# Cross-attention over sixteen batches: the attention product of eleven batches in seven block products, with its sums on GpSimd, and the softmax maximum as bias of the exponential

## The chip, the core and the metric

The kernel runs on one core of a Trainium2 chip. The engines are named as in the profile: PE (TensorE, matmuls), PEld (its weight loads), DVE (VectorE), ACT (ScalarE), POOL (GpSimd) and SP (SyncE, which only issues transfers here). PE writes its results to PSUM, which has eight banks; POOL does not touch PSUM. The metric is device time in microseconds (us), the median of several runs.

## The reference

Everything is in 32-bit floating point. There are 16 batches, 256 queries of 256 features, 77 keys of 192 features, 8 heads of width 256.

```python
Q = (img_embed @ Wq).reshape(B, -1, H, D).transpose(0, 2, 1, 3)
K = (sent_embed @ Wk).reshape(B, -1, H, D).transpose(0, 2, 1, 3)
V = (sent_embed @ Wv).reshape(B, -1, H, D).transpose(0, 2, 1, 3)
score = jnp.einsum('bhqd,bhkd->bhqk', Q, K) / math.sqrt(D)
score = jnp.where(mask, score, -jnp.inf)
attn = jax.nn.softmax(score, axis=-1)
ctx = jnp.einsum('bhqk,bhkd->bqhd', attn, V).reshape(B, -1, H * D)
out = ctx @ Wo + img_embed
mu = jnp.mean(out, axis=-1, keepdims=True)
var = jnp.var(out, axis=-1, keepdims=True)
return (out - mu) * jax.lax.rsqrt(var + EPS) * gamma + beta
```

## The kernel before

**What is multiplied.** The weights are folded once: Wq and Wk of each head into gA and gB (the 192 context features are split into 128 and 64, hence A and B), Wv and Wo into uA and uB. Per group of four batches, g is applied to the context (tiles `pa` in PSUM, copied to `a`), and the scores of a batch are x times a (`ps`). Per batch, u is applied to the context (`pv`, copied to `vw`), and the output is the attention weights times vw (`po`), added to x. Of the 77 keys of a head, 64 go through vw; the last 13 of all heads are packed into one more block, `vr`.

**How it is tiled.** A batch has two tiles of 128 queries; a tile is numbered t, a batch b. Nearly all matmuls in the loop use 32 output columns of the array, so that four of them, one for each quarter of the output's partitions, run together; each is executed in two passes, and the profile counts passes. `attend` (L357) makes `po` of a tile from five terms, four blocks of 128 weights (`pT`, turned by DVE's transpose in `turn`) against 256 columns of vw and one against vr.

**The softmax of a tile.** `shift` (L306): two DVE additions of the mask bias to `ps` give s, a DVE maximum gives top, and POOL subtracts top from s. `exponential` (L324): one ACT exponential of 128x616. `weigh` (L329): a DVE sum and reciprocal, then two POOL multiplications into p (128x512 and 128x104). `turn` (L347): a DVE transpose into pT.

**The layer norm of a tile.** `finish` (L371): DVE adds po to x in place and takes the statistics. `spread` (L383): ACT's square root, which needs another function table than the exponential. `invert` (L390): DVE's reciprocal. `normalise` (L403): two DVE instructions (L416 with gamma, L419 with beta), or, put aside, one on ACT and two on POOL; after the second tile of a batch SP issues the transfer of the output.

**The order.** It is written out by hand: each engine executes its instructions in program order, with semaphores between engines. The loop is software-pipelined over b from -1. An iteration computes the scores of batch b+1 (`new`), prepares vw of b+1 and, up to b = 10, a quarter of the a of the next group, attends for batch b (`now`) and finishes and normalises batch b-1 (`old`). On PE the order is scores, part A of the preparations, part B, attend. On DVE it is finish of old, shift of new, (a transpose of vr), reciprocal, then per tile the sum and the normalisation of an old one, transposes of x in half of the iterations, and turn. On ACT it is the square root, then exponential and copies alternately, then the rest of the copies. All PSUM tiles come from one ring of eight banks (`ps_mm`), taken in program order; an iteration with a takes 4 + 2 + 4 + 2 of them, and a bank is taken again when its reader has let go.

**Set-up.** Before the loop, u is folded from Wv and Wo (`pu`, `pw`), POOL copies four pieces of uB to the other half of the partitions, and after them makes the mask bias ready, for which all shifts wait.

Of the kernel before, what the change touches and what calls it, by code (L numbers as in the profile page):

```python
# [8 lines left out]
F32 = mybir.dt.float32  # L9
I32 = mybir.dt.int32  # L10
AF = mybir.ActivationFunctionType
ALU = mybir.AluOpType
AX = mybir.AxisListType
PSUM = bass.MemoryType.PSUM

P = 128
H = 8
D = 256
EPS = 1e-05
GB = 4  # L20
KM = 64
MASKED = 3.0e38

# [19 lines left out]
def kernel(  # L45
# [13 lines left out]
    nc = tc.nc  # L59
    B, S, DI = x.shape  # L60
    S2, DL = c.shape[1], c.shape[2]
# [3 lines left out]
    NG = B // GB  # L65
# [31 lines left out]

    gB = const.tile([P, NF, DI], F32, tag="gB", name="gB")

    uA = const.tile([P, 2, DI // BK, NF, BK], F32, tag="uA", name="uA")  # L100
    uB = const.tile([P, 2, DI // BK, NF, BK], F32, tag="uB", name="uB")

    cA = const.tile([P, B, S2], F32, tag="cA", name="cA")
    cB = const.tile([P, B, S2], F32, tag="cB", name="cB")
# [16 lines left out]
    def flat(ap):  # L121
        return ap.rearrange("p a b -> p (a b)")

    def half(i):
        return slice(i * LB, (i + 1) * LB)
# [31 lines left out]
    def transpose_x(g, j):  # L157

        cols = xT_of[g][:, j * NM : (j + 2) * NM]
        nc.vector.transpose(cols, cols)  # L160
# [54 lines left out]

    def prepare_vw(b):

        vw_of[b] = vwp.tile([P, 2, 2, DI], F32, tag="vw", name=f"vw_{b}", bufs=3)
        pv = []

        def part_A():
            for k in range(2):
                pv.append(ps_mm.tile([P, 2 * DI], F32, tag="mm", name=f"pv_{b}_{k}"))
                for i in range(NM):
                    nc.tensor.matmul(  # L225
                        pv[k][i * BK : (i + 1) * BK],
                        cA[:, b, k * BK : (k + 1) * BK],
                        uA[:, :, :, i],
                        start=True,
                        stop=False,  # L230
                    )

        def part_B():
            for i in range(NM):
                for k in range(2):
                    nc.tensor.matmul(  # L236
                        pv[k][i * BK : (i + 1) * BK],
                        cB[half(k), b, k * BK : (k + 1) * BK],
                        uB[half(k), :, :, i],
                        start=False,  # L240
                        stop=True,
                    )

        def copies():
            return [
                (vw_of[b][:, :, k, :], pv[k].rearrange("p (e d) -> p e d", e=2)) for k in range(2)
            ]

        return part_A, part_B, copies

    def prepare_last():


        pr = [ps_mm.tile([P, 2, B, KR], F32, tag="mm", name=f"pr_{n}") for n in range(DI // BK)]

        def part_A(e):
            for n, o in enumerate(pr):
                nc.tensor.matmul(  # L258
                    o[:, e].rearrange("p b k -> p (b k)"),
                    flat(uA[:, e, n]),  # L260
                    flat(cRA),
                    start=(e == 0),
                    stop=(e == 1),
                )

        def part_B(e):
            for n, o in enumerate(pr):
                nc.tensor.matmul(  # L268
                    o[:, e].rearrange("p b k -> p (b k)"),
                    flat(uB[half(n % 2), e, n]),  # L270
                    flat(cRB[half(n % 2)]),
                    start=(e == 1),
                    stop=(e == 0),
                )

        part_A(0)
        part_B(0)
        part_B(1)
        part_A(1)
        for n, o in enumerate(pr):  # L280
            to = vr[:, :, n * BK : n * BK + 2 * KR]
            evacuate(to.rearrange("p b (e k) -> p e b k", e=2), o)
# [22 lines left out]

    def shift(t):  # L306

        b, ps = t // QT, ps_of.pop(t)
        s = sp.tile([P, H, S2], F32, tag="s", name=f"s_{t}")
        for a in range(2):  # L310
            nc.vector.tensor_tensor(  # L311
                s[:, a * H // 2 : (a + 1) * H // 2],
                ps[a][:, : H // 2 * S2].rearrange("p (h k) -> p h k", k=S2),
                bias[:, b, :].unsqueeze(1).to_broadcast([P, H // 2, S2]),
                ALU.add,
            )
        top = st.tile([P, H], F32, tag="top", name=f"top_{t}")
        nc.vector.tensor_reduce(top, s, AX.X, ALU.max)  # L318
        nc.gpsimd.tensor_tensor(  # L319
            s, s, top.unsqueeze(2).to_broadcast([P, H, S2]), ALU.subtract  # L320
        )
        s_of[t] = s

    def exponential(t):  # L324
        e = sp.tile([P, H, S2], F32, tag="e", name=f"e_{t}")
        nc.scalar.activation(e, s_of.pop(t), AF.Exp)  # L326
        e_of[t] = e

    def weigh(t):  # L329
# [27 lines left out]
    def attend(t):  # L357
        b, pT = t // QT, pT_of.pop(t)
        po = ps_mm.tile([P, DI], F32, tag="mm", name=f"po_{t}")
        for n in range(NF + 1):  # L360
            for i in range(NM):
                nc.tensor.matmul(  # L362
                    po[i * BK : (i + 1) * BK],
                    pT[:, n, i],
                    vw_of[b][:, n // 2, n % 2, :] if n < NF else vr[:, b, :],
                    start=(n == 0),
                    stop=(n == NF),
                )
        po_of[t] = po

    def finish(t):  # L371
        g, j = t // GT, t % GT
        y = xg_of[g][:, j, :]
        nc.vector.tensor_tensor(y, po_of.pop(t), y, ALU.add)
        bn = st.tile([P, 6], F32, tag="bn", name=f"bn_{t}")
        nc.vector.bn_stats(bn, y)
        if j == 0:
            mv_of[g] = st.tile([P, GT, 2], F32, tag="mv", name=f"mv_{g}", bufs=2)
        nc.vector.bn_aggr(mv_of[g][:, j, :], bn)  # L379
# [3 lines left out]
    def spread(first, last):  # L383

        g, lo, hi = first // GT, first % GT, (last - 1) % GT + 1
        std = st.tile([P, GT], F32, tag="std", name=f"std_{first}")
        nc.scalar.activation(std[:, lo:hi], mv_of[g][:, lo:hi, 1], AF.Sqrt, bias=eps)  # L387
        std_of[first, last] = std
# [45 lines left out]
    with tc.tile_pool(name="wonce", bufs=1) as wp:  # L434
# [32 lines left out]
            load_blocks(wq_blk[:, e], wq_blocks[2 * e + 1])  # L467
        load_c(first, NCR)

        warm = wp.tile([P, 1], F32, tag="warm", name="warm")  # L470
        nc.scalar.activation(warm, eps, AF.Exp)

        wvT = wp.tile([P, NF, NL, P], F32, tag="wvT", name="wvT")
# [208 lines left out]
        for j in range(NF // 2):  # L682
            pu = two_banks("pu", j)
            for a in range(2 * j, 2 * j + 2):
                of_pair(pu, a, wv_part, wo_part)
            for e in range(2):
                evacuate(
                    uA[:, e, :, 2 * j : 2 * j + 2].rearrange("p n a c -> p a n c"),
                    pu[e].rearrange("p a (n c) -> p a n c", c=BK),
                )  # L690
        for j in range(NF // 2):
            for e, pw in enumerate(
                rest_of_pairs(j, (2 * j, 2 * j + 1), wv_part, wo_part, "pw")
            ):
                for i, engine in enumerate((nc.scalar.copy, nc.vector.tensor_copy)):
                    a = 2 * j + i
                    here, there = uB[half(i), e, :, a], uB[half(1 - i), e, :, a]
                    engine(here, pw[half(i)].rearrange("p (n c) -> p n c", c=BK))
                    nc.gpsimd.tensor_copy(there, here)
        nan = wp.tile([P, B, 1], F32, tag="nan", name="nan")  # L700
        nc.vector.tensor_reduce(nan[:, :, 0], bias, AX.X, ALU.max)
        nc.gpsimd.tensor_tensor(nan, nan, nan, ALU.mult)
# [16 lines left out]
    for b in range(-1, B):  # L719
# [2 lines left out]
        new = range((b + 1) * QT, min(b + 2, B) * QT)  # L722
        for t in new:
            scores(t)
        if old and new:
            for t in old:
                finish(t)
            spread(old[0], old[-1] + 1)
        for t in new:
            shift(t)  # L730
        for n in range(0, 2) if b < 0 else range(b + 2, min(b + 3, B // 2)):
            turn_last(n)
        if old and new:
            invert(old[0], old[-1] + 1, aside=b >= B - GB - 1)
        g, n = (b + 1) // GB + 1, (b + 1) % GB
        work = []
        if b + 1 < B:
# [8 lines left out]
        for _, part_B, _ in work:  # L746
            part_B()
        copies = [copy for _, _, of_part in work for copy in of_part()]
        for i, t in enumerate(new):
            exponential(t)  # L750
            for dst, src in copies[i : i + 1]:
                nc.scalar.copy(dst, src)  # L752
        for dst, src in copies[len(new) :]:
            nc.scalar.copy(dst, src)  # L754
        for i, t in enumerate(new):
            weigh(t)
            if old and b < B - 2 and (i or b < B - GB - 1):
                normalise(old[i])
        if g < NG and n >= NF - 2:
            for j in range((n - NF + 2) * GT // 2, (n - NF + 3) * GT // 2, 2):  # L760
                transpose_x(g, j)
        for t in now:
            attend(t)
        for t in new:
            turn(t)
        if B - GB - 1 <= b < B - 2:
            normalise(old[0], aside=True)
        if b == B - 2:
            for i in range(QT):
# [46 lines left out]
```

## Time and profile before

| | us |
|---|---|
| median of 3 runs | 288.15 (286.89 to 288.93) |
| the profiled execution | 285.98 |
| its span, first to last instruction | 284.2 |
| set-up on PE, until the first scores | 57.3 |
| an iteration with a (b = 1 to 10) | 14.5 |
| an iteration without a (b from 11) | 11.4 |
| after the last gap-free matmul, to the end | 16 |

In the profile's rows, a line such as L362 is a line of the kernel, `po<-vw,pT` names the tile written and those read, `128*32` is the rows and columns of the array in use, and `x1024` counts instructions (passes on PE). The second number of a row is the busy time of the group, then the mean of one; the number after the next bar is the time that the engine sat idle before it. In the chain of waits each piece is followed back to what released it. In the table of windows each engine has its busy time and its count.

Other rows that matter, by line and form (busy us, mean ns): the POOL subtraction L319, 128x616, 38.9 and 1216; POOL's products for p, L340, 128x512, 35.4 and 1107; the exponential L326, 23.0 and 719; the 128x512 copies to vw, L752, 18.6 and 581; the 128x308 copies to a, L754, 16.6 and 447.

### The profile page before, as it was taken

Reading aid. Unit: us, or ns where it says so; the run is one execution under the profiler, and the core shown is the slowest. Engines: PE = TensorE matmul, PEld = TensorE weight load, DVE = VectorE, ACT = ScalarE, POOL = GpSimd, SP = SyncE. Lnnn points to the kernel's source line nnn. Section 1 sums busy time; section 2 is a strip of 40 time slices with the busy share of each in tenths; the row PEclk is TensorE's granted clock in tenths of the full one; section 3 lists DMA queues with packets and bytes.
Section 4 is the critical chain, followed back from the end, with each engine's and each line's share of the span. In section 5 each row is a group of like instructions: output and inputs, shape, how many; then the busy total and the mean of one; then the engine's idle time right before and its main releaser. Section 6 shows DMA issues by size and latency. Waiting matters only on the chain.

```text
span 284.2 us, 11523 instructions
## 1 busy us (share of the span) xinstructions
PE 274.4 (97%) x5221; PEld 180.2 (63%) x5221; DVE 215.3 (76%) x421; ACT 115.2 (41%) x199; POOL 119.1 (42%) x150
## 2 busy tenths in 40 slices
PE   8999999999999999999999999999999999999990
PEld 7746599976474747575656565666656567476550
DVE  0245953775777989988888888897978898898883
ACT  3303222214362444453535353535353534725541
POOL 1000069524515252525252434352533437748574
PEclk9999999999999999999999999999999999999998
DMA  6997999960000105920101039301010101010112
GB/s 211 229 224 174 325 213 225 155 142 2 2 6 2 40 2 102 189 86 5 39 2 40 2 81 193 105 2 39 3 39 5 40 3 39 2 42 3 39 40 74
DMA packets 35634, 22.51 MB, mean 79 GB/s; under 512 B 17712, under 2 KB 34048, under 8 KB 35584
## 3 DMA queue, kind: packets, MB, share of 16 engines
q1 hardware_dynamic: 35584, 21.77, 34.8%
q8 instruction: 41, 0.67, 1.0%
q14 instruction: 9, 0.07, 0.1%
HBM read 17.57 MB, written 4.19 MB: 77 GB/s over the span
## 4 chain that ended last, share of the span: by engine, by line
PE 93%; DVE 2%; POOL 1%; ACT 1%; issue 1%; POOLq 0%
PE ps L297 24%; PE po L362 22%; PE pa L184 12%; PE pv L225 10%; PE pa L198 6%; PE pv L236 6%; PE pu L568 3%; PE pr L258 2%; PE pg L611 1%; PE idle L493 1%; PE pw L582 1%; PE pgb L568 1%; PE pr L268 1%; PE pc L545 1%; PE phb L582 1%; PE ph L625 1%
## 5 line engine op out<-in xcount | busy, mean ns | idle before, releaser
L319 POOL TENSOR_TENSOR s<-s,top 128x616 f32<-128x616 f32 x32 | 38.9, 1216 | 90.5 <-DVE top L318 86.0
L297 PE MATMUL ps<-a,xT 128*32 128x154 f32 x2048 | 70.0, 294 | 0.0
L297 PEld LDWEIGHTS ps<-a,xT 128*32 128x32 f32 x2048 | 66.4, 110 | 3.5 <-issue 0.7
L340 POOL TENSOR_TENSOR p<-e,rden 128x512 f32<-128x512 f32 x64 | 50.1, 802 | 31.8 <-ACT a L754 27.0
L362 PE MATMUL po<-vw,pT 128*32 128x256 f32 x1024 | 61.5, 380 | 0.0
L362 PEld LDWEIGHTS po<-vw,pT 128*32 128x32 f32 x1024 | 31.8, 110 | 28.2 <-issue 5.5
L332 DVE TENSOR_REDUCE den<-e 128x8 f32<-128x616 f32 x32 | 25.3, 790 | 23.6 <-ACT e L326 23.6
L184 PE MATMUL pa<-cA,gA 128*32 128x308 f32 x512 | 35.8, 423 | 0.4 <-ACT cA L136 0.4
L326 ACT ACTIVATE e<-s 128x616 f32<-128x616 f32 x32 | 23.0, 719 | 28.7 <-POOL s L319 28.7
L752 ACT COPY vw<-pv 128x512 f32<-128x512 f32 x32 | 18.6, 581 | 36.1 <-PE pv L236 36.1
L311 DVE TENSOR_TENSOR s<-ps,bias 128x308 f32<-128x308 f32 x64 | 27.8, 465 | 4.1 <-PE ps L297 4.1
L225 PE MATMUL pv<-uA,cA 128*32 128x512 f32 x256 | 30.4, 592 | 0.0
L184 PEld LDWEIGHTS pa<-cA,gA 128*32 128x32 f32 x512 | 16.4, 110 | 21.1 <-issue 6.1
L419 DVE SCALAR_TENSOR_TENSOR xg<-xg,rstd,bet 128x256 f32<-128x256 f32 x25 | 27.9, 1117 | 0.9
L387 ACT ACTIVATE std<-mv,eps 128x2 f32<-128x2 f32 (+1 forms) x17 | 5.0, 296 | 55.1 <-DVE mv L379 54.3
L350 DVE STREAM_TRANSPOSE pT<-p 128x640 f32<-128x640 f32 x32 | 25.0, 811 | 2.5 <-POOL p L340 2.5
L318 DVE TENSOR_REDUCE top<-s 128x8 f32<-128x616 f32 x32 | 25.5, 796 | 1.1
L362 PE MATMUL po<-vr,pT 128*32 128x256 f32 x256 | 19.7, 379 | 0.0
L198 PE MATMUL pa<-cB,gB 64*32 64x308 f32 x512 | 19.5, 420 | 0.0
L387 ACT ACT_TABLE_LOAD x15 | 19.2, 1283 | 0.3
L326 ACT ACT_TABLE_LOAD x14 | 18.0, 1283 | 0.3
L236 PE MATMUL pv<-uB,cB 64*32 64x512 f32 x256 | 17.4, 601 | 0.0
(86 smaller groups left out, 272.2 us busy)
## 6 DMA issues: line engine op xcount, KB each, us to landing
xT<-in_x_dram SPq DMA_DIRECT2D x16, 256.0 KB, 7.4
xg<-in_x_dram SPq DMA_DIRECT2D x4, 1024.0 KB, 9.0
out_dram<-xg SPq DMA_DIRECT2D x15, 256.0 KB, 2.2
wo<-in_L_xattn_Wo_dram SPq DMA_DIRECT2D x4, 512.0 KB, 5.4
wvT<-in_L_xattn_Wv_dram SPq DMA_DIRECT2D x16, 96.0 KB, 3.9
wq_nat<-in_L_xattn_Wq_dram SPq DMA_DIRECT2D x2, 512.0 KB, 6.1
wq_blk<-in_L_xattn_Wq_dram SPq DMA_DIRECT2D x8, 128.0 KB, 4.4
wk_blk<-in_L_xattn_Wk_dram SPq DMA_DIRECT2D x8, 96.0 KB, 5.8
```

Source lines behind the costliest of these rows:

```text
L184: nc.tensor.matmul(flat(o[i * BK : (i + 1) * BK]), gA[:, h, cols(dc, i)], flat(cA[:, batches, :]), start=not B_first, stop=B_first,)
L198: nc.tensor.matmul(flat(banks[j + k][i * BK : (i + 1) * BK]), gB[half(k), h % NF, cols(dc, i)], flat(cB[half(k), batches, :]), start=B_fir ...
L225: nc.tensor.matmul(pv[k][i * BK : (i + 1) * BK], cA[:, b, k * BK : (k + 1) * BK], uA[:, :, :, i], start=True, stop=False,)
L236: nc.tensor.matmul(pv[k][i * BK : (i + 1) * BK], cB[half(k), b, k * BK : (k + 1) * BK], uB[half(k), :, :, i], start=False, stop=True,)
L297: nc.tensor.matmul(ps[m // 2][i * BK : (i + 1) * BK, m % 2 * 2 * S2 : (m % 2 + 1) * 2 * S2], xT_of[g][:, j * NM + m, dc], flat(a_of[g][:, ...
L311: nc.vector.tensor_tensor(s[:, a * H // 2 : (a + 1) * H // 2], ps[a][:, : H // 2 * S2].rearrange("p (h k) -> p h k", k=S2), bias[:, b, :]. ...
L318: nc.vector.tensor_reduce(top, s, AX.X, ALU.max)
L319: nc.gpsimd.tensor_tensor(s, s, top.unsqueeze(2).to_broadcast([P, H, S2]), ALU.subtract)
L326: nc.scalar.activation(e, s_of.pop(t), AF.Exp)
L340: nc.gpsimd.tensor_tensor(part, e_mh[:, :, :, keys], rden_mh.unsqueeze(3).to_broadcast(list(part.shape)), ALU.mult,)
L362: nc.tensor.matmul(po[i * BK : (i + 1) * BK], pT[:, n, i], vw_of[b][:, n // 2, n % 2, :] if n < NF else vr[:, b, :], start=(n == 0), stop= ...
L419: nc.vector.scalar_tensor_tensor(y, y, rstd, bet, ALU.mult, ALU.add)
```

## The change

For batches 0 to 10 the two tiles of a batch are multiplied together. Attention weights (two tiles by two halves of the heads) and vw (two halves of the heads by two halves of the output features) are both cut into two by two blocks, and the product is taken by Winograd's form of Strassen's scheme: seven block products instead of eight, and sums before and after.

- Set-up: u gets a fifth block, the combination t2 = b22 - b12 + b11, by four POOL additions of 128x512 placed ahead of the bias. `vw` has four blocks of 128 columns: t2, b21, b22, b11 for these batches, and b21, b22, b11, b12 for the others, at the same 512 columns of matmul.
- `differences` (POOL, one instruction of 128x768) makes t4, t1, t3 of a batch from vw. `sums` (POOL, four of 128x256) makes s1 to s4 from the turned weights.
- `seven` replaces `attend`: four products into bank `pm`, three products and the last keys into bank `po`, all with 128 columns; ACT then copies pm to `m`.
- `add_seven`: DVE adds po to x (moved here from `finish`), and POOL adds m into m twice (128x128) and m into x three times (128x256).
- Softmax, batches 0 to 11: the maximum is taken negated, POOL's subtraction is gone, and the exponential is eight instructions of 128x77, one for each head, with the maximum as bias.
- Order in iterations -1 to 10: DVE takes the shift of new first, and the statistics of old between the sums of new; ACT takes both tiles' exponentials, then the square root, then the copies, the copy of pm, and a small exponential that brings the table back; on DVE then follow the reciprocal, the normalisation of the first old tile, turn, the transposes of x, the normalisation of the second old tile and the additions of po; on POOL p, differences, the additions of m, sums.

```diff
+    def differences(b):
+        vw = vw_of[b].rearrange("p q k d -> p q (k d)")
+        ts = vwp.tile([P, 3, 2, P], F32, tag="ts", name=f"ts_{b}", bufs=2)
+        nc.gpsimd.tensor_tensor(
+            ts.rearrange("p q k d -> p q (k d)"),
+            vw[:, 1:4],
+            vw[:, 0:1].to_broadcast([P, 3, 2 * P]),
+            ALU.subtract,
+        )
+    def sums(b):
...
+        nc.gpsimd.tensor_tensor(s1, a2[0], a2[1], ALU.add)
+        nc.gpsimd.tensor_tensor(s3, a2[0], a1[0], ALU.subtract)
+        nc.gpsimd.tensor_tensor(s2, a2[1], s3, ALU.add)
+        nc.gpsimd.tensor_tensor(s4, a1[1], s2, ALU.subtract)
+    def seven(b):
...
+        def contract(out, *terms):
+            for n, (weight, moving) in enumerate(terms):
+                for i in range(NM):
+                    nc.tensor.matmul(
+                        out[i * BK : (i + 1) * BK],
+                        weight[:, i],
+                        moving,
+                        start=(n == 0),
+                        stop=(n == len(terms) - 1),
+                    )
...
+        contract(pm[:, 0], *block(pT[0][:, 0:2], b11))
+        contract(pm[:, 1], *block(s2, t2))
+        contract(pm[:, 2], *block(s3, t3))
+        contract(pm[:, 3], *block(s1, t1))
+        contract(po[:, 0], *block(pT[0][:, 2:4], b21), last[0])
+        contract(po[:, 1], *block(s4, b22), last[1])
+        contract(po[:, 2], *block(pT[1][:, 2:4], t4), last[2])
+        contract(po[:, 3], last[3])
...
+        nc.scalar.copy(m, pm)
+    def add_seven(b):
...
+        for i in range(QT):
+            add_product(QT * b + i)
+        add(m[:, 1], m[:, 0])
+        add(m[:, 2], m[:, 1])
+        add(y[:, 0], m[:, 0:2])
+        add(y[:, :, 1], m[:, 3:4].to_broadcast([P, QT, P]))
+        add(y[:, 1], m[:, 2:3].to_broadcast([P, 2, P]))
...
-        nc.vector.tensor_reduce(top, s, AX.X, ALU.max)
-        nc.gpsimd.tensor_tensor(
-            s, s, top.unsqueeze(2).to_broadcast([P, H, S2]), ALU.subtract
-        )
+        nc.vector.tensor_reduce(top, s, AX.X, ALU.max, negate=t // QT <= NS)
...
-        nc.scalar.activation(e, s_of.pop(t), AF.Exp)
+            for h in range(H):
+                nc.scalar.activation(e[:, h], s[:, h], AF.Exp, bias=top[:, h : h + 1])
...
+        for u in (uA, uB):
+            t2, _, b22, b11, b12 = (u[:, q].rearrange("p n i c -> p (n i c)") for q in range(5))
+            nc.gpsimd.tensor_tensor(t2, b22, b12, ALU.subtract)
+            nc.gpsimd.tensor_tensor(t2, t2, b11, ALU.add)
...
+        if b < NS:
+            for i, t in enumerate(new):
+                exponential(t)
+                if old:
+                    finish(old[i])
+                weigh(t)
+            if old:
+                spread(old[0], old[-1] + 1)
+            for dst, src in copies:
+                nc.scalar.copy(dst, src)
+            if b + 1 < NS:
+                differences(b + 1)
+            if now:
+                seven(b)
+            nc.scalar.activation(warm, eps, AF.Exp)
+            if old:
+                invert(old[0], old[-1] + 1)
+                normalise(old[0])
+            for t in new:
+                turn(t)
+            if n >= NF - 2:
+                for j in range((n - NF + 2) * GT // 2, (n - NF + 3) * GT // 2, 2):
+                    transpose_x(g, j)
+            if old:
+                normalise(old[1])
+            if now:
+                add_seven(b)
+            if b + 1 < NS:
+                sums(b + 1)
+            continue
```

## The prediction

> **What bounds the kernel now.** I read the page's busy table and 40 slices first, then the chain of waits in order of time, then one loop iteration by engine.
>
> ```profile
> PE 274.4 (97%) x5221; PEld 180.2 (63%) x5221; DVE 215.3 (76%) x421; ACT 115.2 (41%) x199; POOL 119.1 (42%) x150
> ...
> PE   8999999999999999999999999999999999999990
> ...
> DVE  0245953775777989988888888897978898898883
> ```
>
> PE is busy 97% of the span; DVE is next and, inside the loop, near full. A busy PE may still be waiting within its rows, so the chain of waits in order of time decides (start, us, what):
>
> ```profile
> 125.56 4.19 PE ps L297 x128
> 129.74 1.72 PE pv L225 x16
> 131.46 2.07 PE pa L184 x32
> 133.53 1.02 PE pv L236 x16
> 134.55 1.04 PE pa L198 x32
> 135.59 4.45 PE po L362 x80
> 140.04 4.19 PE ps L297 x128
> ```
>
> Each piece begins where the one before ended. One iteration is scores 4.19, preparation 5.85, attend 4.45: 14.48 us, and the chain stays on PE from 16.5 to 268 us. So in the loop a microsecond of matmul is a microsecond of time, and other engines cost nothing until PE waits for them. Their room in one such iteration, from the table of windows:
>
> ```profile
> core 0: us, PE busy (x) PEld busy (x) DVE busy (x) ACT busy (x) POOL busy (x), PEclk, DMA share, GB/s
> 130.00:144.48 14.48, 14.48 (x309) 9.01 (x305) 12.11 (x25) 6.53 (x11) 5.67 (x7) 1.00 0.06 20
> ```
>
> The clock is full (1.00). DVE has 2.4 us to spare, ACT 8, POOL 8.8.
>
> **The change part by part.**
>
> *PE, batches 0 to 10 (the forecast's gain).* A product here is two passes over four column tiles that run together; I call one pass of four a round. Old attend: 2 tiles x 5 terms x 2 passes = 20 rounds of 256 columns (the x80 above). New: seven block products of 2 terms, plus four last-key terms, 18 terms x 2 passes = 36 rounds of 128 columns. Columns fall from 20x256 = 5120 to 36x128 = 4608, rounds rise by 16. Price of a round from the chain: ps 4.19/32 = 0.131 us at 154 columns, pa 2.07/8 = 0.259 at 308, pv 1.72/4 = 0.429 at 512. These lie on 0.417 ns per column plus 2.5 ns, which gives 0.216 at 256 and 0.109 at 128. No column-tiled round of 128 is in this trace; the nearest is a full-array matmul of that width, in the timeline and then in the answer for its tile:
>
> ```profile
> 10.22 1.04 PE L507 MATMUL pt_q<-ident,wq_nat 128*128 128x128 f32 x8
> ```
>
> ```profile
> L507 PEld LDWEIGHTS pt_q<-ident,wq_nat x16: 138/140/144, 6.4 to 10.9; 128*128 128x128 f32 x16
> L507 PE MATMUL pt_q<-ident,wq_nat x16: 272/272/328, 6.4 to 11.0; 128*128 128x128 f32 x16
> ```
>
> Eight in 1.04 us, the last lasting 0.272: (1.04-0.272)/7 = 0.110 apart, although each weight load takes 0.140. The load is thus latency hidden under the matmul before it. Bounds for the new round: 0.109 (streaming) and 0.131 (as fast as ps, should four loads of 0.110 per round not fit in less). I take 0.109, as the nearest row overlaps loads longer than its spacing. Then 36x0.1092 = 3.93 against 20x0.2158 = 4.32 (the other 0.13 of the 4.45 is a gap at the switch from the 64-row tiles and stays): 0.385 us a batch, x11 = **4.2 us**. At 0.131: 4.71, a loss of 0.39x11 = 4.3.
>
> A rule speaks against this. The Trainium skill, "TensorE: Matmul & The Clock Gate", Part 3, says a weight load overlaps running matmuls only when its row group differs. All these tiles use all 128 rows. By that rule a round would be load plus stream, 36x(0.110+0.109) = 7.9 against 20x(0.110+0.216) = 6.5, and the change would lose 1.4 us a batch, 15 in all. But ps rounds of 0.131 with loads of 0.110 leave no room for load plus 0.128 of streaming; the measurement decides.
>
> *Scores, preparation.* The same columns (four of five blocks of 128 instead of two of 256): nothing.
>
> *ACT.* Per tile one exponential (0.719) becomes eight of 128x77 with the bias from a column, up to batch 11. From the 128x2 Sqrt with such a bias (0.296) and 0.69 ns per element ((719-296)/614): 0.348. The four a copies (0.447 each) take 1.38 together, so successors overlap by 0.136: eight cost 1.83, at most 2.78 without overlap. Added too: m copy as the 128x512 vw copy, 0.58, and the small Exp, 0.2, which only moves the table load (1.28) off the path. Per batch 6.5 - 1.4 + 3.7 + 0.8 = 9.6, at most 11.5, of 14.0.
>
> *POOL.* Gone: two subtractions, 2.43. New: dense additions, nearest rows the 128x256 gam product, 0.73 undisturbed, and the 128x1232 bias addition, 2.25. So 256 columns 0.73, 128 some 0.5, 768 between 1.5 and 2.2 (I take 1.8). Differences 1.8, sums 4x0.73 = 2.9, additions 2x0.5 + 3x0.73 = 3.2: 7.9. Per batch 5.5 + 5.5 = 11 of 14.
>
> *DVE.* The same instructions in another order: shift 1.58 a tile, BN 0.56, den with reciprocal 0.95, transpose 0.75, po addition 0.4, two x transposes 1.22 in half of the iterations, one vr transpose 0.63 in the early ones. The pair of statistics products needs a second look, in the answers for its two lines:
>
> ```profile
> L419 DVE SCALAR_TENSOR_TENSOR xg<-xg,rstd,bet x25: 518/1156/1158, 89.6 to 279.4; 128x256 f32<-128x256 f32 x25
> ...
> L416 DVE SCALAR_TENSOR_TENSOR xg<-xg,mv,gam x25: 431/434/958, 89.2 to 278.4; 128x256 f32<-128x256 f32 x25
> ```
>
> Same form, 0.434 and 1.156: L419 runs beside POOL's p product (1.107). The Trainium skill, "SBUF — State Buffer", section Who interferes with whom, says a DVE instruction with two SBUF inputs and a POOL instruction that reads SBUF exclude each other for a whole instruction. The trace's price for one meeting is 0.72; by the rule meeting the differences would cost up to 1.8. I price a pair at 0.9 free, 1.6 as now.
>
> *Does PE ever wait?* New iteration, 0 = start of scores, products from 10.17 to 14.10 (4.19+5.85+0.13+3.93). DVE shifts to about 5.5. ACT: exponentials 3.5 to 7.4, Sqrt with table load to 9.0 (its wait for the statistics, done at 7.5, has the six copies behind it), copies to 11.5, m copy 12.5 (pm complete at 11.9; the small Exp and the next exponentials stand behind it). POOL: p to 10.2, differences to 12.1, then the m additions. DVE: den 7.5 to 8.5, rstd 9.1, first pair to 10.7, turns to 12.1, x transposes 13.4, second pair 14.3, po addition (waits for the last product) to 15.2. Behind it stands the next shift, whose first bank is full at 15.2. Behind POOL's wait for that addition stand y additions to 17.5 and sums to 20.5; PE needs the first sum at 24.7. The po bank is needed by pa at 20.5, the copied vw and a banks from 14.1 to 18.3 against 11.5. So every wait of PE is met 2 to 5 us early. The DVE to ACT to DVE loop is 13.3 us in iterations with x transposes, 12.1 in others; with the high exponential and both pairs contended some 15 and 14.
>
> *Set-up.* Four POOL additions 128x512, 1.1 to 1.5 each, 5 in all, push the bias from 54.3 to 59.3; the first shift began at 58.6 and its second half waited until 59.6. Next late would be turn 1 (71.2) for attend 0 (77.6): hidden. Were it not, each microsecond counts once.
>
> *SP.* The output transfer goes from mid-iteration to its end; loads for the next group stand behind it, but have two iterations (28 us) against 7.4 to land: nothing. Iterations from 11 on keep their operations and 11.4 us; the tail from 268 is untouched.
>
> Sum: 284.2 - 4.2 = 280.0 span, 281.8 with the 1.8 around it (285.98 - 284.2). The profiled run lies 2.2 below the median of the runs, 288.15, so I subtract from the median: **283.9**.
>
> **The rivals.**
>
> *Rounds do not shrink in full.* 128-column rounds limited by loads or by the feeding of 288 instructions in 3.9 us (13.6 ns each; ps shows 16.4). At 0.116 to 0.119 the batch saves 0.03 to 0.14 us, 0.4 to 1.5 in all: 286.6 to 287.8. For: ps loads are busy 66.4 of 70.0 us. Against: pt_q above, and ps lying exactly on the line. A part of it stands for "change does not deliver": 0.2.
>
> *DVE's loop becomes the period (slower).* Place: the second statistics pair and the po addition, just before the next shift, with POOL now holding the port 11 of 14 us. PE has 24.7-20.5 = 4.2 us of lead to lose over 11 iterations, then waits. A 1% loss needs 11x(L-14.1)-4.2 > 4.2+2.9, that is L over 15.1. If each pair meets the differences and exponentials do not overlap, L is about 15.5: 11x1.4-4.2 = 11.2, net 7, 295. For: DVE is at 12 of 14, and nearly every L419 now meets POOL. Against: x transposes are in half of the iterations only, and the exponential must be at its high end. Chance 0.14 with rounds at 0.131 (292) inside it.
>
> *More than that:* PE has no idle to recover; only the shorter way out of the last batches could, 1 us: 0.04.
>
> **How the numbers follow.** The forecast has 0.62, partial rounds or short waits 0.20, slower 0.14, better 0.04. One per cent is 2.9 us, about what runs spreading over 2.0 us can tell from none. Of the forecast, a tenth falls within 1% by the spread of the runs; some of the partial case reaches faster. So faster 0.63, same 0.24, slower 0.13. Range: down to 282.5 (spread of the runs), up to 289.5 across the partial case; above it some 0.14 remain, below it 0.05.
>
> **What would show it.** Right: PE without gaps through the loop, 128-column rounds 0.109 apart, product piece near 4.06, iteration near 14.1, eight exponentials near 1.8, DVE's shift still waiting for PE. Wrong: PE idle before scores or the sums product with DVE or POOL as releaser; L416/L419 over 1.2 mean; rounds of 0.12 or more.

## The result, and the profile after

The changed kernel takes 284.61 us (median of 4 runs, 284.28 to 285.26) against 287.52 for the kernel before, measured beside it (4 runs, 286.76 to 288.93): a ratio of 0.990, 95% interval 0.985 to 0.994. In a second series (8 and 13 runs) it was 284.76 against 286.99, ratio 0.9925, 0.9895 to 0.9955. So it is faster by 2.2 to 2.9 us; 4.2 were forecast. The profiled execution took 285.26 and has a span of 283.5.

From the page of the kernel before, the chain by engine; then from that of the changed kernel, the busy table and the chain by engine:

```profile
PE 93%; DVE 2%; POOL 1%; ACT 1%; issue 1%; POOLq 0%
```

```profile
PE 271.2 (96%) x5925; PEld 196.8 (69%) x5925; DVE 207.5 (73%) x421; ACT 156.8 (55%) x390; POOL 179.6 (63%) x240
...
PE 77%; DVE 11%; POOL 4%; DMA 2%; ACT 2%; issue 2%; POOLq 0%; SPq 0%
```

PE's busy time fell by 3.2 us while its instructions rose by 704 (64 passes for each of 11 batches). But PE's share of the chain fell from 93% to 77%: a stretch at the end now belongs to DVE, POOL and ACT.

First the loop. One iteration in the chain of waits of the changed kernel (start, us, what), the same place as the one shown for before:

```profile
139.87 4.19 PE ps L313 x128
144.06 1.72 PE pv L241 x16
145.77 2.07 PE pa L199 x32
147.85 1.02 PE pv L252 x16
148.87 1.04 PE pa L213 x32
149.90 1.88 PE pm L436 x64
151.79 2.18 PE po L436 x80
153.97 4.19 PE ps L313 x128
```

It has no gap. Scores and preparation last what they did; attend's 4.45 has become 1.88 + 2.18 = 4.06, and the iteration 14.10 instead of 14.48. The row of this iteration in the table of windows (PE, PEld, DVE, ACT, POOL, clock, DMA share, GB/s):

```profile
139.87:153.97 14.10, 14.10 (x376) 10.35 (x372) 12.14 (x25) 10.08 (x28) 10.87 (x14) 1.00 0.07 22
```

ACT rose from 6.5 to 10.1 and POOL from 5.7 to 10.9, as priced, and DVE stayed at 12.1. PE still waits for none of them.

Now the sum over stretches. From the first scores to those of iteration b = 11, the eleven products of seven lying between, the kernel before takes 169.67 us (57.30 to 226.97). The changed kernel takes 165.69 (58.78 to 224.47), and 165.4 to 165.8 in another profile of it and in those of two versions that share this stretch. That is a gain of 3.9 to 4.3: the forecast 4.2. From the scores of iteration 11 to the end of the span, before takes 57.2 (284.2 - 226.97) and after 59.0 (283.5 - 224.47; 59.1 in its second profile). **1.8 us are lost there.** Inside that stretch the chain of waits of the changed kernel reads:

```profile
224.47 4.23 PE ps L313 x128
228.73 0.49 DVE s L328
229.24 0.80 DVE top L335
...
230.93 0.19 DVE mv L494
231.15 0.30 ACT std L502
231.51 1.25 issue
232.75 0.73 ACT e L346
```

This is iteration b = 11, the first without a product of seven ahead, and the first whose `shift` is followed by the statistics of both old tiles (`finish`) at once. The chain leaves PE at 228.73 and doesn't come back to it. The 1.25 of "issue" is a load of the function table, as ACT's timeline of the same kernel shows (start, us, line, operation, and in brackets the idle time before it with its releaser):

```profile
231.15 0.29 ACT L502 ACTIVATE std<-mv,eps 128x2 f32<-128x2 f32 x1 [5.31 <-DVE mv L494]
231.46 1.28 ACT L346 ACT_TABLE_LOAD   x1
232.75 0.72 ACT L346 ACTIVATE e<-s 128x616 f32<-128x616 f32 x1
```

ACT takes the square root ahead of the exponentials here, as before. But its input, the statistics, now stands behind both shifts on DVE. The exponential's own input was ready at 229.24 (POOL's subtraction for it, 228.02 + 1.22). It starts at 232.75.

The exponential is thus held up by 3.5 us. DVE, from its shift to its next shift, needs 14.96 us here (225.59 to 240.55) where before needed 11.39 (229.94 to 241.33). Not all of this is delay: the interval holds the statistics of two batches, since they stand behind the shift in iteration 11 and ahead of it in 12. What counts is how far DVE's first addition lies behind PE's scores of the same iteration. In iteration 12, from the timelines of PE and DVE, first of the kernel before and then of the changed one:

```profile
238.16 4.37 PE L297 MATMUL ps<-a,xT 128*32 128x154 f32 x128
241.33 0.83 DVE L311 TENSOR_TENSOR s<-ps,bias 128x308 f32<-128x308 f32 x2
```

```profile
235.67 4.37 PE L313 MATMUL ps<-a,xT 128*32 128x154 f32 x128
240.55 0.83 DVE L328 TENSOR_TENSOR s<-ps,bias 128x308 f32<-128x308 f32 x2
```

DVE is 3.17 us behind PE before and 4.88 after: 1.7 us late. This isn't made up later, because DVE's own loop in the last iterations, its waits for the exponentials included, is 11.28 us long (251.84 to 263.12 from first addition to first addition) against PE's 11.38. A delay of DVE shrinks by 0.1 us in each, and in iteration 14, the last with scores, DVE is 3.00 behind PE before and 4.70 after: still 1.7 late. PE itself loses nothing until the last two products, where it waits 0.5 us for pT; the delay comes out at the end, when DVE, ACT and POOL finish the last batch.

### The profile page after: what moved, and what is told of

The parts are those of the page before. It is cut to its first block, busy times and chain, and to the rows that moved or that the text cites. A ratio compares the mean times of both kernels' runs of the same rounds, so it can differ in the third digit from the quotient of the medians.

```text
span 283.5 us, 13229 instructions
## 1 busy us (share of the span) xinstructions
PE 271.2 (96%) x5925; PEld 196.8 (69%) x5925; DVE 207.5 (73%) x421; ACT 156.8 (55%) x390; POOL 179.6 (63%) x240
## 4 chain that ended last, share of the span: by engine, by line
PE 77%; DVE 11%; POOL 4%; DMA 2%; ACT 2%; issue 2%; POOLq 0%; SPq 0%
PE ps L313 19%; PE pa L199 12%; PE po L436 9%; PE pv L241 7%; PE pm L436 7%; PE pa L213 6%; PE pv L252 4%; PE pu L683 3%; PE pr L274 2%; DMA wq_nat<-in_L_xattn_Wq_dram 2%; DVE top L335 2%; DVE s L328 2%; DVE bn L491 2%; DVE pT L373 2%; POOL p L363 1%
## 5 line engine op out<-in xcount | busy, mean ns | idle before, releaser
L349 ACT ACTIVATE e<-s,top 128x77 f32<-128x77 f32 x192 | 50.3, 346 | 42.9 <-DVE top L335 40.7
L363 POOL TENSOR_TENSOR p<-e,rden 128x512 f32<-128x512 f32 x64 | 46.7, 752 | 27.3 <-DVE rden L357 24.2
L328 DVE TENSOR_TENSOR s<-ps,bias 128x308 f32<-128x308 f32 x64 | 29.7, 473 | 14.8 <-PE ps L313 13.1
L469 POOL TENSOR_TENSOR xg<-xg,m 128x256 f32<-128x256 f32 x33 | 24.2, 733 | 13.8 <-DVE xg L483 12.1
L199 PEld LDWEIGHTS pa<-cA,gA 128*32 128x32 f32 x512 | 17.0, 110 | 20.5 <-issue 7.0
L671 POOL COPY cB<-cB 64x224 f32<-64x224 f32 (+1 forms) x6 | 1.9, 358 | 37.3 <-DVE cB L153 37.3
L399 POOL TENSOR_TENSOR ts<-vw 128x768 f32<-128x768 f32 x11 | 22.0, 2001 | 0.0
L385 PE MATMUL po<-vw,pT 128*32 128x256 f32 x320 | 19.2, 380 | 0.5 <-DVE pT L373 0.5
L213 PEld LDWEIGHTS pa<-cB,gB 64*32 64x32 f32 x512 | 9.7, 107 | 11.3 <-issue 7.6
L337 POOL TENSOR_TENSOR s<-s,top 128x616 f32<-128x616 f32 x8 | 9.7, 1217 | 12.2 <-DVE top L335 11.0
L385 PEld LDWEIGHTS po<-vw,pT 128*32 128x32 f32 x320 | 10.3, 110 | 10.0 <-DVE s L328 2.5
L531 DVE SCALAR_TENSOR_TENSOR xg<-xg,mv,gam 128x256 f32<-128x256 f32 x25 | 16.8, 671 | 0.0
```

Of the source, the lines that this page charges most:

```text
L199: nc.tensor.matmul(flat(o[i * BK : (i + 1) * BK]), gA[:, h, cols(dc, i)], flat(cA[:, batches, :]), start=not B_first, stop=B_first,)
L213: nc.tensor.matmul(flat(banks[j + k][i * BK : (i + 1) * BK]), gB[half(k), h % NF, cols(dc, i)], flat(cB[half(k), batches, :]), start=B_fir ...
L328: nc.vector.tensor_tensor(s[:, a * H // 2 : (a + 1) * H // 2], ps[a][:, : H // 2 * S2].rearrange("p (h k) -> p h k", k=S2), bias[:, b, :]. ...
L349: nc.scalar.activation(e[:, h], s[:, h], AF.Exp, bias=top[:, h : h + 1])
L363: nc.gpsimd.tensor_tensor(part, e_mh[:, :, :, keys], rden_mh.unsqueeze(3).to_broadcast(list(part.shape)), ALU.mult,)
L385: nc.tensor.matmul(po[i * BK : (i + 1) * BK], pT[:, n, i], vw_of[b][:, 2 - n // 2 * 2 : 4 - n // 2 * 2, n % 2, :] if n < NF else vr[:, b, ...
```

## The experiments

The kernel before took 287.46 us (10 runs, 285.94 to 288.36) beside the first four of these kernels (runs 1 to 4), and 286.99 (13 runs) beside the other four. Ratios are to these.

**1. Exponentials first in iteration 11.** Theory: the 1.8 us are the square root standing ahead of the exponentials in the transition.

```diff
         if b == NS:
             for t in old:
                 finish(t)
-            spread(old[0], old[-1] + 1)
...
-        if b >= NS and new:
+        if b > NS and new:
             invert(old[0], old[-1] + 1, aside=True)
...
         for i, t in enumerate(new):
             weigh(t)
+            if b == NS and i:
+                spread(old[0], old[-1] + 1)
+                invert(old[0], old[-1] + 1, aside=True)
```

> In iteration 11 alone, both exponentials go ahead of the square root on ACT (the changed kernel has them behind it). Theory A, that the missing part of the gain is a delay on ACT in iteration 11 which DVE then carries through five iterations into the tail: the first exponential starts at about 4.8 us into the iteration instead of 8.3, DVE waits for PE again in iteration 12, and the time falls by 1.5 to 1.8 us, to about 283. Theory B, that the iterations without a are held by DVE's own work (11.3 us) whatever the start: unchanged within 0.3 us. Theory C, that what is missing lies in the set-up (scores begin 1.5 us later in the profile): unchanged.

Measured: 283.5 us (4 runs, 283.31 to 284.23), ratio 0.989 (0.985 to 0.9925). That is 1.1 below the changed kernel. ACT's timeline of this kernel, in the same iteration:

```profile
228.47 0.72 ACT L346 ACTIVATE e<-s 128x616 f32<-128x616 f32 x1 [4.74 <-POOL s L337]
230.69 0.59 ACT L904 COPY vw<-pv 128x512 f32<-128x512 f32 x1 [1.50 <-PE pv L252]
231.17 0.72 ACT L346 ACTIVATE e<-s 128x616 f32<-128x616 f32 x1
...
233.68 0.30 ACT L502 ACTIVATE std<-mv,eps 128x2 f32<-128x2 f32 x1
```

The first exponential now starts when POOL's subtraction lands. The second doesn't: a copy of vw stands ahead of it and waits 1.50 us for PE. DVE did not wait for PE again in the next iteration, so that part of the expectation failed (nor does it in the kernel before). DVE waits 0.69 us for the second exponential and 1.05 for the square root, and its shift to shift fell to 13.86 only. In iteration 12 it is 3.78 us behind PE (234.87 to 238.65): 1.1 less than in the changed kernel, 0.6 more than in the kernel before. The stretch from the scores of iteration 11 to the end is 57.9. The square root's place explains 1.1 of the 1.8; 0.7 were still open.

**2. The old product in the new order.** Is the loop's gain the 36 short rounds, or does something else of the change bring it?

```diff
-        parts = slice(0, 4) if b < NS else slice(1, 5)
+        parts = slice(1, 5)
...
-            if b + 1 < NS:
-                differences(b + 1)
-            if now:
-                seven(b)
+            for t in now:
+                attend(t)
...
-            if now:
-                add_seven(b)
-            if b + 1 < NS:
-                sums(b + 1)
+            for t in now:
+                add_product(t)
```

> The changed kernel with the old product of two times 40 matmuls of 256 columns in all batches, without sums, differences and additions; softmax and order stay new. Theory A, that all of the gain in the loop is the 36 narrow rounds in place of 20 wide ones: iteration 14.48 us, time 284.6 + 11 x 0.385 = 288.8, a little above the kernel before because the delay of iteration 11 stays. Rival, that part of the gain comes from the new order or softmax: below 287.

Measured: 289.4 us (7 runs, 288.34 to 291.19), ratio 1.008 (1.005 to 1.012). The iteration is that of before again; its product in the chain of waits of this kernel, and the scores after it:

```profile
137.25 4.45 PE po L385 x80
141.71 4.19 PE ps L313 x128
```

From the first scores to those of iteration 11 it takes 169.67 us (58.96 to 228.63), as the kernel before does, and from there to the end 59.0, as the changed kernel does. So all of the loop's gain is the product. Softmax and order alone make the kernel 1.9 us slower than before (289.4 - 287.46), which is the 1.8 lost in the transition, seen without the gain on top.

**3. POOL's subtraction of the maximum kept.** What would the product of seven cost if the maximum were not the bias of the exponential?

```diff
-        nc.vector.tensor_reduce(top, s, AX.X, ALU.max, negate=t // QT <= NS)
-        if t // QT > NS:
+        nc.vector.tensor_reduce(top, s, AX.X, ALU.max)
+        if True:
             nc.gpsimd.tensor_tensor(
...
-        if t // QT > NS:
+        if True:
             nc.scalar.activation(e, s, AF.Exp)
```

> The changed kernel with the old softmax everywhere: POOL subtracts the maximum, one exponential per tile. Theory A, that POOL could not carry sums and subtractions in one iteration since the subtractions queue behind the sums and everything of the softmax behind them: the loop of POOL, ACT and DVE is about 16 us, PE waits, time 293 to 300. Rival, that only the busy time counts (11 + 2.4 = 13.4 of 14.1): 284 to 286.

Measured: 295.6 us (4 runs, 295.38 to 295.86), ratio 1.030 (1.027 to 1.0335), 11.0 above the changed kernel. POOL's timeline of this kernel shows where the subtractions come to stand:

```profile
129.87 2.36 POOL L469 TENSOR_TENSOR xg<-xg,m 128x256 f32<-128x256 f32 x3
...
134.49 0.73 POOL L419 TENSOR_TENSOR ss<-pT,ss 128x256 f32<-128x256 f32 x1
135.19 2.38 POOL L337 TENSOR_TENSOR s<-s,top 128x616 f32<-128x616 f32 x2
```

They run last in a row of 7.7 us without a pause (129.87 to 137.57), behind the additions to x of the product before and the sums for the next one, so the exponentials begin at 136.43 after 7.0 us of idle ACT. DVE's iterations last 14.8 or 15.8, 15.26 on average over eight: the loop was expected near 16, the time is inside the expected 293 to 300. PE's waits appear where they were absent: 1.9 us of the old product for pT, 3.4 of the scores for a copy of vw. Taking the subtraction off POOL is no side issue of the change: in this order of POOL's work the product of seven needs it. Subtractions ahead of the sums were not tried.

**4. Statistics and square root in the old places, in all iterations.**

```diff
-        if old and new and b > NS:
+        if old and new:
             for t in old:
                 finish(t)
             spread(old[0], old[-1] + 1)
...
-        if b == NS:
-            for t in old:
-                finish(t)
-            spread(old[0], old[-1] + 1)
...
                 exponential(t)
-                if old:
-                    finish(old[i])
                 weigh(t)
-            if old:
-                spread(old[0], old[-1] + 1)
```

> The changed kernel with the old place of the statistics and the square root: finish of the old batch ahead of the shifts, square root ahead of the exponentials, in all iterations. Theory A, that the new order is needed because POOL's additions to y are ready only 3.5 us into the iteration: DVE stands still until then, the shifts come 3.6 us later, its loop is some 15 to 16 us, PE loses its lead and waits, time 290 to 296. Rival, that the order is indifferent since DVE has 2 us to spare: 283 to 285.

Measured: 308.8 us (308.32 to 309.11), ratio 1.076 (1.073 to 1.080). The direction is as expected, the size is not: 24.2 us above the changed kernel, where 5 to 11 were expected. On DVE the statistics wait for POOL's last addition to x, and the shift of the next scores stands behind them; from DVE's timeline of this kernel:

```profile
149.11 0.74 DVE L483 TENSOR_TENSOR xg<-po,xg 128x256 f32<-128x256 f32 x2
151.18 0.43 DVE L491 BATCH_NORM_STATS2 bn<-xg 128x6 f32<-128x256 f32 x1 [1.33 <-POOL xg L469]
...
152.54 0.83 DVE L328 TENSOR_TENSOR s<-ps,bias 128x308 f32<-128x308 f32 x2
```

And on ACT the table of the exponential is loaded only after DVE's maximum, although its row names no tile that it reads. ACT's timeline of this kernel, and then that of the kernel before at such a place:

```profile
146.41 1.28 ACT L502 ACT_TABLE_LOAD   x1
152.66 0.29 ACT L502 ACTIVATE std<-mv,eps 128x2 f32<-128x2 f32 x1 [4.97 <-DVE mv L494]
154.30 1.28 ACT L349 ACT_TABLE_LOAD   x1 [1.34 <-DVE top L335]
155.59 4.11 ACT L349 ACTIVATE e<-s,top 128x77 f32<-128x77 f32 x16
```

```profile
230.05 0.30 ACT L387 ACTIVATE std<-mv,eps 128x2 f32<-128x2 f32 x1 [4.24 <-DVE mv L379]
230.37 1.28 ACT L326 ACT_TABLE_LOAD   x1
232.99 0.72 ACT L326 ACTIVATE e<-s 128x616 f32<-128x616 f32 x1 [1.34 <-POOL s L319]
```

Before, the load followed the square root at once and was over before POOL began its subtraction (231.74). Here it starts 1.34 us after the square root has ended, and its 1.28 us lie between the maximum and the exponentials. So two things were lost at once, and the next run parts them.

**5. Only DVE's part of that.** Statistics ahead of the shift as in run 4, but the square root stays behind the exponentials up to iteration 10. From iteration 11 on this kernel is run 4, and with it has before's order at the transition.

```diff
-        if old and new and b > NS:
+        if old and new:
             for t in old:
                 finish(t)
-            spread(old[0], old[-1] + 1)
+            if b >= NS:
+                spread(old[0], old[-1] + 1)
...
-        if b == NS:
-            for t in old:
-                finish(t)
-            spread(old[0], old[-1] + 1)
...
-                if old:
-                    finish(old[i])
```

> In the iterations with seven block products DVE takes the statistics of old ahead of the shift of new, as the kernel before did, while the square root on ACT stays behind the exponentials. Against the run with both in the old places (308.8, loop 16.97) it tells DVE's order from ACT's. Theory A: most of the loss is DVE waiting, ahead of its shift, for POOL's additions of m: the loop is near 16.3 us and the time 300 to 303. Rival: the place of the square root with its table load was the whole of it, and DVE's order alone costs little: loop 14.1 to 14.4, time 284 to 287.

Measured: 297.45 us (4 runs, 297.31 to 297.77), ratio 1.036 (1.032 to 1.040). It lies 2.6 below the expected range and 10 above the rival's, 11.35 below run 4 and 12.7 above the changed kernel. DVE's shift to shift is 14.87 or 15.86 (132.91, 147.78, 163.64), 15.4 on average, where 16.3 was expected; run 4 has 16.1 and 17.0. DVE's timeline of this kernel:

```profile
146.41 0.43 DVE L491 BATCH_NORM_STATS2 bn<-xg 128x6 f32<-128x256 f32 x1 [1.32 <-POOL xg L469]
...
153.69 0.80 DVE L355 TENSOR_REDUCE den<-e 128x8 f32<-128x616 f32 x1 [0.96 <-ACT e L349]
...
155.30 0.17 DVE L509 RECIPROCAL rstd<-std 128x2 f32<-128x2 f32 x1 [0.58 <-ACT std L502]
```

DVE has 11.5 or 12.5 us of work in an iteration (the difference is the transposes of x) and now waits 1.5 for POOL, 1.0 for the exponentials and 0.6 for the square root. Its loop is past PE's 14.10 and sets the time. DVE's order alone costs 12.7 us; the place of the square root with its table costs 11.35 more on top of it. What that place would cost with DVE's order left as changed was not run, so the two figures hold for this sequence only.

**6 to 8. The changed kernel, run 1's version, and one more, side by side.** The open 0.7 us were put down to DVE's loop of 11.28 us from iteration 12 on, which keeps a delay. The third kernel is run 1's, and both old tiles of a batch are normalised on ACT and POOL there instead of one of them on DVE; that takes a pair of 0.43 + 1.16 us a batch off DVE.

```diff
-            if old and b < B - 2 and i:
-                normalise(old[i])
...
         if b < B - 2:
-            normalise(old[0], aside=True)
+            for t in old:
+                normalise(t, aside=True)
```

> The changed kernel once more, beside the version with the exponentials first, to compare the two in one call. Theory A (the 1.1 us between them is the transition into iteration 11): about 284.6, and 1.1 to 1.5 over the other version. Theory B (the 1.1 is the spread between calls): the two within 0.5 of each other. If first scores of this run start earlier than the 58.78 of its last profile, the loop itself (first scores to scores of b = 11) should again save 4.0 to 4.3 us against the 169.7 of the kernel before.

> The version with iteration 11's exponentials ahead of the square root, again. Theory A: 283.5, 1.1 to 1.5 below the changed kernel in this call. Theory B: within 0.5 of it.

> As the version with the exponentials first, and from iteration 11 on both old tiles of a batch are normalised on ACT and POOL instead of one of them on DVE. Theory A: from iteration 12 DVE's own loop of 11.28 us carries the delay of the transition to the end, since PE's 11.38 recovers only 0.1 an iteration; without the 1.6 us pair DVE's loop falls to about 9.7, the chain goes back to PE within one iteration, and the time is 0.3 to 0.7 below the version with the exponentials first (283.0 or so). Rival: POOL, with two further 128x256 pairs an iteration (8.9 of 11.4 us busy), delays p or the last output, and the time is the same or up to 1 us longer.

Measured: the changed kernel 284.76 (8 runs, 284.09 to 286.22); exponentials first 283.65 (6 runs, 283.1 to 284.0), ratio 0.988 (0.985 to 0.9915); both tiles aside 282.94 (6 runs, 282.29 to 283.73), ratio 0.985 (0.982 to 0.989). The first step is 1.1 us for the place of the square root, again. The second, 0.7 for the work taken off DVE, is small against the spread (the ranges of the two versions overlap), but the profiles have it too: 57.9 and 57.3 from the scores of iteration 11 to the end. The chain by engine of the last kernel, and then its end in order of time:

```profile
PE 91%; DVE 2%; DMA 2%; POOL 2%; ACT 1%; issue 1%; POOLq 0%; SPq 0%
```

```profile
257.75 4.19 PE ps L313 x128
261.93 1.72 PE pv L241 x16
263.65 1.13 PE pv L252 x16
...
265.24 0.73 ACT e L346
```

The chain is back on PE up to 264.78, where it was on DVE from 228.73 in the changed kernel. The stretch from the scores of iteration 11 to the end is 57.3, as in the kernel before (57.2). POOL, at 8.4 to 9.1 us of 11.4 in iterations 12 to 14, now lets DVE wait 0.85 us for p, but this doesn't reach PE: that rival is out. One thing this run doesn't part: it also takes the pair off iteration 11 itself, and in iteration 12 DVE is only 2.66 us behind PE (234.81 to 237.47). So the delay is gone by then, and was not worked off in later iterations. This version takes 4.05 us less than before (286.99 - 282.94): what the loop alone brings.

## Why the prediction was right, and where 1.8 us of it went

*The forecast's gain: right to the hundredth.* The round of 128 columns was put at 0.109, between 0.109 and 0.131. A product piece of 4.06 and an iteration of 14.1 were forecast; the trace has 4.06 and 14.10, and run 2 shows that nothing but the product brings it. One figure of the working is off by two: the four prices lie on 0.834 ns per column (0.131 us at 154, 0.429 at 512), not on 0.417; the 0.216 and 0.109 that were used go with 0.834, so no sum changes. The answer for the tile `pm`, changed kernel (minimum, median and maximum in ns):

```profile
L436 PEld LDWEIGHTS pm<-ts,ss x352: 110/110/110, 79.8 to 221.9; 128*32 128x32 f32 x176
L436 PE MATMUL pm<-ts,ss x352: 272/273/273, 79.9 to 222.0; 128*32 128x128 f32 x176
```

Sixteen rounds of `pm` take 1.88 us, 0.1175 by the piece, with the switch from the 64-row tiles at its start in it; the twenty of `po` take 2.18, 0.109 each. Each round has four loads of 0.110 each, so they run beside matmuls and beside each other. The rule of the Trainium skill that was weighed ("TensorE: Matmul & The Clock Gate", Part 3: overlap only where the row group differs; another sentence of that Part allows it for the background weight buffer too) would have made it 15 us slower. All these tiles use all 128 rows, and the trace shows their loads hidden; no run here can tell whether by that buffer.

*The other engines' timetable: right within 0.7 us.* In the iteration above, counted from its start at 139.87, forecast and measured: exponentials to 7.4 and 7.8, square root to 9.0 and 9.4, copies to 11.5 and 11.6, copy of pm to 12.5 and 12.7, p to 10.2 and 10.8, differences to 12.1 and 12.8. From the start of the iteration before it (125.77), the po addition to 15.2 and 14.9, additions to x to 17.5 and 17.0, sums to 20.5 and 20.0. The eight exponentials were put at 1.83 and took 2.1 (16 in 4.20): the overlap of neighbours was taken from the copies, and there is less of it here. It stayed within the bound of 2.78 and cost nothing in the loop.

*DVE beside POOL.* A pair of statistics products was priced at 0.9 free and 1.6 contended. In the rows of the changed kernel (busy us, mean ns, idle before):

```profile
L531 DVE SCALAR_TENSOR_TENSOR xg<-xg,mv,gam 128x256 f32<-128x256 f32 x25 | 16.8, 671 | 0.0
L534 DVE SCALAR_TENSOR_TENSOR xg<-xg,rstd,bet 128x256 f32<-128x256 f32 x25 | 14.2, 568 | 0.9
```

The pair fell to 1.24 from before's 1.59 (0.474 + 1.117), though POOL is busy nearly twice as long in an iteration (10.9 us against 5.7). In the iteration above, the first pair begins in the last part of POOL's products for p (1.02 for L531, then 0.49 for L534), the transposes fall beside the 2.05 us of differences, and the second pair (0.45 and 0.48) falls where POOL waits for the po addition. What counts is which instructions meet, not how busy POOL is. The second rival (DVE's loop as the period) got its time from pairs that all meet POOL's longest instruction; in this order they don't.

*DVE's loop can become the period all the same,* by another way than the rival's. In runs 3, 4 and 5 it is the period, at 15.3, 16.5 and 15.4 us, because DVE waits for POOL and ACT, not because its pairs are slow. The changed kernel escapes this since the maximum is no longer subtracted on POOL and the statistics stand after the shift.

*The set-up: hidden, as said.* The four additions take 1.27 each, the bias ends at 60.94 (58.69 + 2.25) where 59.3 was forecast (1.5 of the difference is the later start of the whole, see below), the first shift waits 1.57 for it, and PE waits for none of it in the chain.

*The step that failed:* "Iterations from 11 on keep their operations and 11.4 us; the tail from 268 is untouched." They keep their operations, but iteration 11 doesn't keep its order: statistics after both shifts, and the square root still ahead of the exponentials. DVE leaves it 1.7 us late. The square root's place is 1.1 us of that (runs 1 and 7); the other 0.7 go when DVE has less to do from there on (run 8). Almost nothing of it is made up, since DVE's loop of 11.28 us has only 0.1 of slack against 11.38: 1.7 late in iteration 12, 1.7 in iteration 14. The prediction counted DVE's slack where it was 2 us and did not look at the stretch where it was 0.1. With it the gain would have been put at 4.2 - 1.8 = 2.4; 2.2 to 2.9 were measured.

*A part of the closeness is luck.* The time of 283.9 was forecast from a median of 288.15 for the kernel before. Measured beside the changed kernel it took 287.52, so the time was missed by 0.7 us only, where the gain was missed by 1.3.

*What stays open.* First scores begin at 57.8 to 59.0 us in the profiles of changed kernels and at 57.30 in the one profile of before. The difference arises ahead of the folding of u: `pu` starts at 36.82 before and at 38.29 after, and from there both take 20.5 us to the first scores. The diff leaves the loads and products of that first part as they were. In the changed kernel PE waits 0.5 us there for the landing of the first weights (5.63 us), which before's chain does not show; run 7 begins at 57.76 without that wait. Before's profile is that of one of its fastest runs (285.98), and the medians leave little room for a systematic loss (4.05 of gain with the tail mended, against 3.9 to 4.3 in the loop), but it wasn't tried by itself.

## What to carry to other kernels

Where the matmul engine is the bound and a column costs what it costs, fewer columns pay even at more, smaller products, as long as the loads still hide (0.109 us a round of 128 columns with four loads of 0.110). The sums go to an engine with room, but make that room first: leaving one POOL operation of 1.2 us a tile in place, behind the sums, cost 11 us. And when an order is changed for most iterations, walk through the first iteration that keeps the old one: a waiting instruction there may stand ahead of one whose input has long been ready, and an engine with 0.1 us of slack an iteration carries such a delay to the end.

## What was not expected of the hardware

- A function-table load can wait for the data of the instruction behind it, but not every one does. In run 4 the load ahead of the exponentials started 1.34 us after the square root had ended, released by DVE's maximum. In the same run the load ahead of the square root (146.41) ran 5 us before the statistics were there, and in the kernel before the load ahead of the exponential (230.37) was over before POOL began to subtract (231.74). The loads that waited stand ahead of an exponential with the maximum as bias; why these wait stays open. The small exponential on a constant, which the change puts after the copy of pm, loads the table with nothing to wait for.
- PE's weight loads once paused in the changed kernel with nothing to wait for that the profile shows. In its timeline, in the second block of `po` of one batch:

```profile
124.08 0.22 PEld L436 LDWEIGHTS po<-vw,ss 128*32 128x32 f32 x8 [0.19 <-issue]
```

  That iteration lasted 14.38 instead of 14.10. Loads of x had kept the DMA engines 79% busy up to 123, but from 124 to 125 these moved nothing. Run 1 has no such hole in that batch, with as many loads, and a loop shorter by 0.28 (165.41). Run 8 has one of 0.27 in another batch (181.38). The cause is open.
- A dense POOL addition took 0.73 us at 128x256, 1.27 at 128x512 and 2.0 at 128x768, so 0.5 to 0.7 for each 256 columns: nearly in proportion, and the guess of 1.8 for the last was low.
